# Down projection of a fused adaLN block: eight of its eleven pieces moved to float32r, with the widening of h on ScalarE

## The chip, the cores and the metric

The kernel runs on one core of a Trainium2 chip. The metric is the device time of one execution in microseconds, the median of several runs. The core has TensorE (PE in the profile; PEld is its loading of stationary operands), VectorE (DVE), ScalarE (ACT), GpSimd (POOL) and SyncE (SP). Each works through its own queue of instructions in order; transfers are issued from SP's or GpSimd's queue.

## The reference

The input x is two sequences of 4096 rows of 512 numbers (8192 rows in all). A transformer block is applied: a modulated layer norm, a gated linear recurrence over the sequence (the "attention" part), then a second modulated layer norm and a feed-forward part with 1408 inner columns. Every operand of the feed-forward matrix products is rounded to four bits in blocks of 16 along the contracted dimension.

```python
def fp4_linear(x, w):
    xq = fp4_quant_dequant(x)     # per block of 16: scale = max|x| / 6, value = grid[...] * sign * scale
    wq = fp4_quant_dequant(w)
    return einsum('bsk,nk->bsn', xq, wq)

h = layernorm(x) * (1 + ca) + sa
x = x + ga * attn(h)                                     # h @ W, sigmoid, scan along n, q * y
h = layernorm(x) * (1 + cb) + sb
gate, y = fp4_linear(h, w_gate), fp4_linear(h, w_up)     # 512 -> 1408 each
x = x + gb * fp4_linear(silu(gate) * y, w_down)          # 1408 -> 512
```

The six modulation rows sa, ca, ga, sb, cb, gb come from a small product of the condition vector c; there is one set for each of the two sequences (batches).

## The kernel before

The program has two phases. The first (0 to about 528 us) does the attention part, and beside it rounds the feed-forward weights and lays them in SBUF transposed: `wgT` and `wuT` (gate and up) and `wdT` (down). Every weight and every activation is held as two float16 parts, a high and a low one, and a product of two such numbers is made in passes of TensorE: three float16 passes (high x high, high x low, low x high; the list `PASSES`), or two passes where one part is made so that less is lost (the list `TWO`: high x high and low x low, with parts that are mixed by a factor, `LAM` or `LAMX`).

The second phase (528 us to the end) goes over `NT` = 64 tiles of 128 rows. The order of all instructions on every engine is the order in which the loop at the end writes them (`tc.manual_schedule`). Names below are those of `before.py`.

- `products(i)` (line 1069): gate and up of tile i. There are three column groups of 480, 464 and 464, each for two matrices, into six PSUM banks. The contracted 512 columns are four chunks of 128. `twos(i)` of these chunks are done in two passes with float32r weights (`wide`) and float32r activations (`xw`), the others in three float16 passes (`held` or `wgT`/`wuT`, with `x2T`). `twos` is 0 for the first tiles and climbs to 3 by one chunk every two tiles: tiles 5 and 6 have one, 7 and 8 two, later ones three. A group takes 12, 11, 10 or 9 passes accordingly, products 72, 66, 60 or 54.
- `down(i - LAG)`, with `LAG` = 2 (line 1190): the down product of the tile before last. The 1408 inner columns are eleven chunks ("pieces") of 128. The first eight take three float16 passes and the last three two (with `LAM`); this makes 30 passes of 512 columns into one of two side banks (`sd`). The stationary operand is h, transposed (`hT`); `wdT` streams.
- VectorE and ScalarE turn the products into h and quantise it. `silu` (line 1086, ScalarE) and `gated` (line 1091, VectorE) read the banks; VectorE's three gated products free them. Then follow the block maxima (`h_max`), the bounded scales (`sb`), a reciprocal of 88 columns, `h_unit` (division by the scale on VectorE, absolute values on ScalarE, line 1147), `h_round` (lines 107 and 109), and the parts. The first 1024 columns of h get theirs by one multiplication of the rounded integers with two spread scales (`h_spread` on ScalarE, line 1153, and line 1170 on VectorE); the last 384 get them by value: a multiplication (line 1164), a high part on ScalarE (line 1166), a low part (line 1176). One transpose on SP's queue writes `hT`.
- Between these steps lie those of later tiles: x of tile i + 2 is divided, rounded and transposed (`x_unit`, `x_round`, `x_low`; the transpose writes `x2T`), x of tile i + 3 is normalised (`x_hat` on ScalarE, `x_times` on GpSimd, `x_plus` on VectorE, its maximum and `x_scales`), and the statistics of tile i + 4 are taken (`mean_x`, `spread_x`, `x_off`). GpSimd also does the small scale steps (`total`, `h_scales`, `h_parts`).
- The output: `out_of` (line 1241, ScalarE) scales the side bank and frees it, `out_times` (line 1246, GpSimd) multiplies by gb, and `send` (line 1232) adds the result to the output in DRAM by a transfer on GpSimd's queue.
- At tile 0, `move_weights` (line 1018) copies gate and up weights to `held` in eight moves of 704 KB on SP's queue. From tile 2 to tile 7 one job per tile turns a half chunk (1408 columns) of them into float32r: `widen_sum` on VectorE, `widen_high` on ScalarE, `widen_low` on VectorE. The jobs for the chunks 3, 2 and 1 follow one another; `widen_rows` (line 1050, ScalarE) widens x.
- The start: x of tiles 0, 1 and 2 is brought on ahead in the slots of phase 1 (`EARLY`, `LATE`, `x_early` with its stages 0 to 3). The end: at tile 62 no down is queued; at tile 63 down(60) and down(61) stand behind products(63), then follow down(62) and `last_down(63)` in halves of 256 columns.

Of the kernel before, what the change touches and what calls it, by code (L numbers as in the profile page):

```python
# [19 lines left out]
P = 128  # L20
D = 512
# [23 lines left out]
LAM = 81.0  # L45
LAMX = 101.0
TWOS = 3
MOVED = 2


@with_exitstack
def tile_adaln_block(
# [62 lines left out]
    def bounded(engine, am, nb):  # L115
        sb = small.tile([P, nb], F32, name="sb", tag=f"sb{nb}", bufs=2)
        engine.tensor_scalar(sb, am, 6e-12, TIE / 6.0, ALU.max, ALU.mult)  # L117
        return sb
# [11 lines left out]
    def inverse(sb, nb):  # L130
        inv = small.tile([P, nb], F32, name="inv", tag=f"inv{nb}", bufs=2)
        V.reciprocal(inv, sb)
        return inv
# [272 lines left out]
    DOWN = [(k, *p) for k in range(IC) for p in (PASSES if k * P < HSPLIT else TWO)]  # L406
# [122 lines left out]
    def quant_weight(wt, am, col, parts, hl):  # L529
# [17 lines left out]
        for at, by in parts:  # L547
            if by is None:
                A.copy(b1[:, at], xn[:, at])
            else:  # L550
                A.activation(b1[:, at], xn[:, at], AF.Copy, scale=by)
# [3 lines left out]
    def quant_rows(wt, i, am, col):  # L555
        dst = weights(("wgT", "wuT")[col], col, [P, 2 * KC, INTER])
        hl = new_hl()
        yield from quant_weight(wt, am, col, [(slice(0, D), None)], hl)
        S.dma_start_transpose(dst[:, :, i * P : (i + 1) * P], flat(hl))
# [6 lines left out]
    def quant_down(wt, i, j):  # L566
# [5 lines left out]
        by = None if n0 < HSPLIT else (LAM - 1.0) / LAM  # L572
        yield from quant_weight(wt, am_d[i][j], 2, [(slice(0, w), by)], two)
# [52 lines left out]
    NS = NBLK * KC  # L626
    qx, x1s, xst, gbs = {}, {}, {}, {}
    mods = {}

    def mods_for(b):  # L630
        if b not in mods:
            mods[b] = (mod_load(4, b, f"mod_c{b}"), mod_load(3, b, f"mod_s{b}"))
        return mods[b]
# [13 lines left out]
    def spread_x(x1, nm):  # L647
        sq = work.tile([P, D], BF16, name="sq", tag="sq", bufs=1)
        ss = small.tile([P, 1], F32, name="vs", tag="vs")
        A.activation(sq, x1, AF.Square, bias=nm, accum_out=ss)  # L650
        rstd = small.tile([P, 1], F32, name="rstd", tag="rstd", bufs=10)
# [3 lines left out]

    def stats_x(x1):
        return spread_x(x1, mean_x(x1))

    def twos(i):
        return min(max((i - MOVED - 1) // 2, 0), TWOS)  # L660

# [10 lines left out]
    def x_scales(h, am):  # L672
        sb = bounded(G, am, NBX)
# [3 lines left out]
        return h, sb, st, u  # L677

    def x_unit(h, sb, st, u):
        xn = work.tile([P, D], F32, name="xn", tag="xn512", bufs=1)  # L680
        V.tensor_tensor(blocks(xn), blocks(h), spread(inverse(sb, NBX), NBX), ALU.mult)
        A.activation(h, xn, AF.Abs, scale=MAGIC)
        return h, xn, st, u
# [17 lines left out]

    ahead = {}

    def x_early(i, stage):
        if stage == 0:
            ahead[i] = x_scales(*x_norm(i))
        elif stage == 1:
            ahead[i] = x_unit(*ahead[i])
# [4 lines left out]

    EARLY = {NS - 3: [(0, 1)], NS - 2: [(0, 3), (1, 1)], NS - 1: [(1, 3)]}
    LATE = {NS - 4: [(0, 0)], NS - 3: [(0, 2), (1, 0)], NS - 2: [(1, 2)], NS: [(2, 0)]}

# [184 lines left out]
    with order:  # L901
# [3 lines left out]
        for slot in range(KC, NS + 3):  # L905
# [83 lines left out]
            if NS - 5 <= slot < NS - 1:  # L989
                n = slot - NS + 5  # L990
                xst[n] = stats_x(x1s[n])
            for n, stage in LATE.get(slot, []):
                x_early(n, stage)
            gate = cur
    tc.no_sync_barrier()
# [35 lines left out]
    def widen_sum(k, m):  # L1031
        hi, lo = moved[k][m]
        cv = ring.tile([P, INTER], F32, name="cv", tag="xnh")
        V.tensor_tensor(cv, hi, lo, ALU.add)
        return k, m, cv

    def widen_high(k, m, cv):
        A.copy(wide[k][m][0], cv)
        A.activation(cv, cv, AF.Copy, scale=LAMX)

    def widen_low(k, m, cv):
        b1, b2 = wide[k][m]
        V.scalar_tensor_tensor(out=b2, in0=b1, scalar=1.0 - LAMX, in1=cv, op0=ALU.mult, op1=ALU.add)

    def widen_rows(i):
        n = twos(i)
        if n:
            x2T = qx[i][0]
            xw = gring.tile([P, 2, n, P], F32R, name="xw", tag="xw", bufs=2)
# [29 lines left out]

    def brief():  # L1080
        return gring.tile([P, D], F32, name="silu", tag="silu", bufs=3)
# [18 lines left out]
    def x_off(i):  # L1100
        nm, rstd = xst[i]
        off = small.tile([P, 1], F32, name="off", tag="off")
        G.tensor_tensor(off, nm, rstd, ALU.mult)
        xst[i] = rstd, off

    def x_hat(i):
        rstd, off = xst.pop(i)
        h = x1s.pop(i)
        A.activation(h, h, AF.Identity, bias=off, scale=rstd)
        return i, h  # L1110

    def x_times(i, h):
        scale, by = mods_for(i * P // N)
        xm = brief()
        G.tensor_tensor(xm, h, scale, ALU.mult)
        return h, xm, by

    def x_plus(h, xm, by):
        V.tensor_tensor(h, xm, by, ALU.add)
# [4 lines left out]
    hb = HSPLIT // QB  # L1124

    def h_max(hid):
        am = small.tile([P, NBH], F32, name="amh", tag="amh", bufs=1)
        block_max(am, hid)
        return hid, bounded(V, am, NBH)

    def h_scales(sb):
        rt, u = total(sb, NBH, ud, 1)
        sl = small.tile([P, NBH], F32, name="sl", tag=f"sl{NBH}", bufs=2)
        G.tensor_scalar(sl[:, hb:], sb[:, hb:], rt, WPEAK * LAM, ALU.mult, ALU.mult)  # L1134
        G.tensor_scalar(sl[:, :hb], sb[:, :hb], rt, None, ALU.mult)
        return rt, sl, u

    def h_parts(sb, rt, sl):
        sh = small.tile([P, hb], BF16, name="sh", tag="shh", bufs=2)
        A.activation(sh, sb[:, :hb], AF.Copy, scale=rt)  # L1140
        G.tensor_tensor(sl[:, :hb], sl[:, :hb], sh, ALU.subtract)
        return sh

    def h_unit(hid, sb):
        xn = ring.tile([P, INTER], F32, name="xn", tag="xnh")
        V.tensor_tensor(blocks(xn), blocks(hid), spread(inverse(sb, NBH), NBH), ALU.mult)  # L1146
        A.activation(hid, xn, AF.Abs, scale=MAGIC)  # L1147
        return xn

    def h_spread(sh, sl):  # L1150
        se = ring.tile([P, 2, HSPLIT], F16, name="se", tag="se")
        for n, src in enumerate((sh, sl[:, :hb])):
            A.activation(blocks(se[:, n, :]), spread(src, hb), AF.Copy, scale=WPEAK)
            yield se
# [7 lines left out]
    def h_value(xn, nq, sl):  # L1162
        v = xn[:, HSPLIT:]
        V.tensor_tensor(blocks(v), blocks(nq[:, HSPLIT:]), spread(sl[:, hb:], NBH - hb), ALU.mult)
        hl = ring.tile([P, 2, INTER], F16, name="hhl", tag="hhl")
        A.activation(hl[:, 0, HSPLIT:], v, AF.Copy, scale=1.0 / LAM)
        return v, hl

    def h_low(i, nq, v, hl, se, u):
        V.tensor_tensor(  # L1170
            hl[:, :, :HSPLIT],
            nq[:, :HSPLIT].unsqueeze(1).to_broadcast([P, 2, HSPLIT]),
            se,
            ALU.mult,
        )
        V.scalar_tensor_tensor(
            out=hl[:, 1, HSPLIT:],
            in0=hl[:, 0, HSPLIT:],
            scalar=1.0 - LAM,
            in1=v,  # L1180
            op0=ALU.mult,
            op1=ALU.add,
        )
        hT = ring.tile([P, 2 * IC, P], F16, name="hT", tag="hT", bufs=2)
        S.dma_start_transpose(hT, flat(hl))
        qh[i] = hT, u

    def down_part(hT, pd, d):
        for n, (k, hp, wp) in enumerate(DOWN):
            T.matmul(  # L1190
                pd,
                hT[:, hp * IC + k, :],
                wdT[:, wd_chunk(wp, k), d],
                start=n == 0,
                stop=n == len(DOWN) - 1,
            )

    def down(i):
        hT, u = qh.pop(i)
        pd = side((P, D))  # L1200
        down_part(hT, pd, slice(0, D))
        return i, pd, u

    def last_down(i):

        hT, u = qh.pop(i)
        b, t0 = divmod(i * P, N)
        o = new_out()
        for n in range(2):
            d = slice(n * D // 2, (n + 1) * D // 2)  # L1210
            pd = bank(n)[:, : D // 2]
            down_part(hT, pd, d)
# [166 lines left out]
```

## Time and profile before

| | us |
|---|---|
| median of 3 runs | 1700.97 (1698.98 to 1703.94) |
| profiled execution | 1701.52 |
| its span | 1699.7 |
| phase 1, 0 to 528.6: busy PE / DVE / ACT / POOL | 526.7 / 442.1 / 399.3 / 297.9 |
| tiles 0 to 9, 528.6 to 719.2 (190.6) | 187.6 / 172.4 / 124.5 / 102.8 |
| tiles 10 to 61, 719.2 to 1643.8 (924.6) | 924.6 / 841.0 / 607.9 / 511.1 |
| the end, 1643.8 to 1699.7 (55.9) | 48.9 / 34.7 / 18.5 / 13.0 |

The span is one execution on the core; the profiled execution's own time is 1.8 us longer. A row of the profile names the line, the engine, the operation, the written and read tiles, their shapes and the number of instructions, then the busy time in us, the mean of one in ns, the idle time of that engine just before them and what ended it. Here float32r operands appear as f32 (matrix products) or fp32r (casts). In the chain of waits each row is a stretch of work on the path that ended last; in a timeline a row is a run of like instructions on one engine, with the idle time before it in brackets.

### The profile page before, as it was taken

Reading aid. Unit: us, or ns where it says so; the run is one execution under the profiler, and the core shown is the slowest. Engines: PE = TensorE matmul, PEld = TensorE weight load, DVE = VectorE, ACT = ScalarE, POOL = GpSimd, SP = SyncE. Lnnn points to the kernel's source line nnn. Section 1 sums busy time; section 2 is a strip of 40 time slices with the busy share of each in tenths; the row PEclk is TensorE's granted clock in tenths of the full one; section 3 lists DMA queues with packets and bytes.
Section 4 is the critical chain, followed back from the end, with each engine's and each line's share of the span. In section 5 each row is a group of like instructions: output and inputs, shape, how many; then the busy total and the mean of one; then the engine's idle time right before and its main releaser. Section 6 shows DMA issues by size and latency. Waiting matters only on the chain.

```text
span 1699.7 us, 24145 instructions
## 1 busy us (share of the span) xinstructions
PE 1687.7 (99%) x8089; PEld 944.2 (56%) x8089; DVE 1490.2 (88%) x1927; ACT 1150.2 (68%) x2295; POOL 924.8 (54%) x1277
## 2 busy tenths in 40 slices
PE   9999999999999999999999999999999999999998
PEld 6444444444444445565666666666666566665664
DVE  7767889899985999998989989899898998998985
ACT  6676787788875667766666666666666666666652
POOL 5554555566654455655555555555555555555532
PEclk9999999999999999999999999999999999999999
DMA  7799979999976534445444444444444444444444
GB/s 249 177 243 218 201 184 204 186 206 199 207 153 183 114 70 82 80 81 95 97 93 86 78 95 78 88 86 83 95 78 83 89 83 94 79 80 94 73 82 72
DMA packets 471453, 208.92 MB, mean 123 GB/s; under 512 B 426470, under 2 KB 427750, under 8 KB 471328
## 3 DMA queue, kind: packets, MB, share of 16 engines
q1 hardware_dynamic: 456496, 173.85, 48.5%
q0 software_dynamic: 14544, 33.52, 11.1%
q8 instruction: 63, 1.03, 0.2%
q14 instruction: 62, 0.51, 0.1%
q10 hardware_dynamic: 288, 0.01, 0.0%
HBM read 62.86 MB, written 33.58 MB: 57 GB/s over the span
## 4 chain that ended last, share of the span: by engine, by line
PE 94%; DMA 2%; DVE 2%; ACT 1%; issue 1%; POOL 0%; DVEq 0%; POOLq 0%; SPq 0%; ACTq 0%
PE mm L1069 43%; PE mm L417 27%; PE sd L1190 23%; DMA gmax<-gsum 1%; DMA hT<-hhl 1%; DMA xT<-hl 0%; PE mm L1190 0%; PE mm L819 0%; DMA x2T<-hl 0%; ACT sq L370 0%; PE sd L220 0%; PE sd L234 0%; DVE ld L158 0%; ACT hl L383 0%; DVE xn L107 0%
## 5 line engine op out<-in xcount | busy, mean ns | idle before, releaser
L1069 PE MATMUL mm<-wide,xw 128*128 128x464 f32 (+1 forms) x2052 | 553.9, 403 | 0.0
L417 PE MATMUL mm<-xT,wqT 128*128 128x512 f16 (+1 forms) x2340 | 498.4, 376 | 0.8 <-DMA xT<-hl 0.8
L1069 PEld LDWEIGHTS mm<-wide,xw 128*128 128x128 f32 x2052 | 386.5, 188 | 72.5
L1190 PE MATMUL sd<-wdT,hT 128*128 128x512 f16 x1890 | 418.7, 379 | 1.7 <-DVE o L1221 1.7
L417 PEld LDWEIGHTS <-wqT 128*128 128x128 f16 x2340 | 228.6, 98 | 270.3 <-issue 1.7
L1069 PE MATMUL mm<-held,x2T 128*128 128x464 f16 (+1 forms) x1386 | 337.4, 365 | 3.0 <-DMA x2T<-hl 3.0
L1190 PEld LDWEIGHTS <-hT 128*128 128x128 f16 x1950 | 186.0, 98 | 226.8 <-issue 15.1
L1069 PEld LDWEIGHTS <-x2T 128*128 128x128 f16 x1530 | 126.3, 98 | 169.2 <-issue 71.1
L1091 DVE SCALAR_TENSOR_TENSOR hid<-mm,u,silu 128x464 f32<-128x464 f32 (+1 forms) x192 | 128.8, 701 | 79.4 <-PE mm L1069 69.3
L125 POOL TENSOR_TENSOR rt<-rms,mone 128x1 f32<-128x1 f32 x128 | 72.9, 569 | 221.7 <-ACT asb L123 221.7
L1147 ACT ACTIVATE hid<-xn 128x1408 f32<-128x1408 f32 x64 | 88.1, 1377 | 114.4 <-DVE xn L1146 114.4
L1086 ACT ACTIVATE silu<-mm,u 128x464 f32<-128x464 f32 (+1 forms) x192 | 116.3, 644 | 34.0 <-PE mm L1069 32.9
L453 ACT COPY yh<-y 128x1024 uint16<-128x1024 uint16 x64 | 66.9, 1045 | 68.8 <-DVE y L446 58.1
L652 POOL TENSOR_SCALAR rstd<-vs 128x1 f32<-128x1 f32 x118 | 25.2, 213 | 161.0 <-ACT sq L650 160.4
L107 DVE SCALAR_TENSOR_TENSOR xn<-hid,xn 128x1408 f32<-128x1408 f32 x64 | 103.6, 1619 | 2.9 <-ACT hid L1147 2.9
L1146 DVE TENSOR_TENSOR xn<-hid,inv 128x1408 f32<-128x1408 f32 x64 | 104.0, 1626 | 2.2
L136 DVE TENSOR_REDUCE amh<-hid 128x88 f32<-128x1408 f32 x64 | 103.7, 1620 | 2.2
L123 ACT ACTIVATE asb<-sb 128x88 f32<-128x88 f32 (+1 forms) x128 | 31.3, 245 | 107.9 <-DVE sb L117 105.1
L109 DVE SCALAR_TENSOR_TENSOR nq<-hid,xn 128x1408 f16<-128x1408 f32 x64 | 103.6, 1618 | 0.1
L1246 POOL TENSOR_TENSOR silu<-o,mod 128x512 f32<-128x512 f32 x32 | 41.2, 1288 | 100.3 <-DVE hid L1091 100.3
L435 DVE TENSOR_TENSOR_SCAN y<-sig,cy,mm 128x512 f32<-128x512 f32 x56 | 71.1, 1269 | 24.5 <-PE mm L417 21.2
L1134 POOL TENSOR_SCALAR sl<-sb,rt 128x24 f32<-128x24 f32 x64 | 88.3, 1379 | 6.3
(153 smaller groups left out, 2727.3 us busy)
## 6 DMA issues: line engine op xcount, KB each, us to landing
ld<-out_dram SPq DMA_DIRECT2D x65, 256.0 KB, 2.9
xr<-in_L_attn_x_dram SPq DMA_DIRECT2D x64, 256.0 KB, 3.7
out_dram<-xr POOLq DMA_DIRECT2D x64, 256.0 KB, 3.5
out_dram<-silu POOLq DMA_DIRECT2D x60, 256.0 KB, 4.0
scratch<-in_L_wmod_dram SPq DMA_DIRECT2D x24, 256.0 KB, 4.7
ld<-in_L_ffn_w_gate_dram SPq DMA_DIRECT2D x22, 256.0 KB, 3.1
ld<-in_L_ffn_w_up_dram SPq DMA_DIRECT2D x22, 256.0 KB, 3.3
ld<-in_L_ffn_w_down_dram SPq DMA_DIRECT2D x16, 256.0 KB, 3.5
```

The costliest lines, as they stand in the source:

```text
L107: V.scalar_tensor_tensor(out=xn, in0=a, scalar=FLOOR, in1=xn, op0=ALU.max, op1=ALU.add)
L109: V.scalar_tensor_tensor(out=nq, in0=a, scalar=FLOOR, in1=xn, op0=ALU.max, op1=ALU.subtract)
L125: G.tensor_tensor(rt, rms, mone[:, :1], ALU.pow)
L136: V.tensor_reduce(am, src.rearrange("p (b k) -> p b k", k=QB), AX.X, ALU.max, apply_absolute_value=True)
L417: T.matmul(pp[:, t], wqT[e][:, wp, k, part, :], xT[:, xp * KC + k, t], start=n == 0, stop=n == 3 * KC - 1,)
L1069: T.matmul(pp[:, : n1 - n0], x2T[:, xp * KC + k, :] if k < k0 else xw[:, xp, k - k0, :], (rows_of(i, m, k) if k < k0 else wide[k][m])[wp][ ...
L1086: A.activation(sl[:, :w], pairs[j][0][:, :w], AF.Silu, scale=u[:, 0:1])
L1091: V.scalar_tensor_tensor(out=hid[:, n0:n1], in0=pairs[j][1][:, : n1 - n0], scalar=u[:, 1:2], in1=sl[:, : n1 - n0], op0=ALU.mult, op1=ALU.mult,
L1134: G.tensor_scalar(sl[:, hb:], sb[:, hb:], rt, WPEAK * LAM, ALU.mult, ALU.mult)
L1146: V.tensor_tensor(blocks(xn), blocks(hid), spread(inverse(sb, NBH), NBH), ALU.mult)
L1147: A.activation(hid, xn, AF.Abs, scale=MAGIC)
L1190: T.matmul(pd, hT[:, hp * IC + k, :], wdT[:, wd_chunk(wp, k), d], start=n == 0, stop=n == len(DOWN) - 1,)
```

## The change

The change touches the second phase.

- Down: for the first `DWIDE` = 7 tiles it is 33 float16 passes (eleven pieces, three passes each). From tile 7 on the last three pieces take three float16 passes (9, first in order) and the first eight take two float32r passes each (16), with `LAMX`. The stationary operand h of these eight is widened from float16 to float32r on ScalarE (`widen_h`, 128 x 2048 columns), queued right behind the absolute values of the following tile's h. There is one buffer, `hwT`.
- The down weights of the eight pieces are widened too: the widening jobs become eleven (`wide_jobs`), two per tile, and end in tile 7. Three of them store their result to DRAM (`far`), and `fetch_far`, on GpSimd's queue at the end of tile 8, brings five pieces (2.5 MB) back into the room of `wdT` (`near`); the three float16 pieces are copied aside before (`keep_rest`, 768 KB, on SP's queue).
- The ways in which h's parts are made are swapped: the first 1024 columns go by value (two multiplications, two high parts on ScalarE, two subtractions), the last 384 by spread scales. Two transposes (`hvT`, `hrT`) replace one. ScalarE's high parts stand last in its order of a tile.
- h's and x's scales share one tile (`cell`) and one reciprocal. The shift addition of x moves from VectorE to GpSimd. The small steps of GpSimd are reordered (`total` and `h_scales` ahead of `rstd_x` and `x_off`, the sending of the output later); `squares_x` moves ahead on ScalarE, `x_unit` ahead of `h_unit`, and both steps of `h_round` stand together, ahead of `x_low`.
- `twos` climbs by one chunk per tile: tile 4 has one, tile 5 two, tile 6 and later three. `xw` has one buffer in place of two.
- The modulation rows of batch 1 are loaded into the tiles of batch 0, at tile 29 (gb at tile 16).
- The start: x of tile 2 passes two more stages in phase 1's extra slot, and its last stage is queued right behind products(0), ahead of `move_weights`. The end: at tile 63 only down(60) is queued up front; tiles 61 and 62 are widened on ScalarE before tile 63's sums, and tile 63 after the outputs.

```diff
-    DOWN = [(k, *p) for k in range(IC) for p in (PASSES if k * P < HSPLIT else TWO)]
...
     def twos(i):
-        return min(max((i - MOVED - 1) // 2, 0), TWOS)
+        return min(max(i - MOVED - 1, 0), TWOS)
...
+    def fetch_far():
+        t = ctile([P, 5, 2, D], F32R, "near", tag="weights2")
+        n = 0
+        for f in far:
+            w = f.shape[1]
+            G.dma_start(t[:, n : n + w], f)
+            n += w
+        for j in range(5):
+            wide_d[2 + j] = [t[:, j, part, :] for part in range(2)]
+
+    def wide_jobs():
+        for k, m in ((3, 0), (3, 1), (2, 0), (2, 1)):
+            yield half(k, m)
+        yield pieces(6, 1, far[2])
+        for m in range(2):
+            yield half(1, m)
+        yield pieces(2, 2, far[0])
+        yield pieces(7, 1, None)
+        yield pieces(4, 2, far[1])
+        yield pieces(0, 2, None)
...
-            xw = gring.tile([P, 2, n, P], F32R, name="xw", tag="xw", bufs=2)
+            xw = gring.tile([P, 2, n, P], F32R, name="xw", tag="xw")
...
-        xm = brief()
-        G.tensor_tensor(xm, h, scale, ALU.mult)
-        return h, xm, by
-
-    def x_plus(h, xm, by):
-        V.tensor_tensor(h, xm, by, ALU.add)
+        G.tensor_tensor(h, h, scale, ALU.mult)
+        G.tensor_tensor(h, h, by, ALU.add)
+        return h
...
+    def h_value(i, xn, nq, sl):
+        by = (LAMX - 1.0) / LAMX if i >= DWIDE else 1.0
+        hl = ring.tile([P, 2, HSPLIT], F16, name="hv", tag="hv")
+        for n, at in enumerate(HALVES):
+            b = slice(n * HB // 2, (n + 1) * HB // 2)
+            V.tensor_tensor(blocks(xn[:, at]), blocks(nq[:, at]), spread(sl[:, b], HB // 2), ALU.mult)
+            A.activation(hl[:, 0, at], xn[:, at], AF.Copy, scale=by)
+        return hl
...
+    def h_low(i, xn, hl, hrT, u):
+        for at in HALVES:
+            V.tensor_tensor(hl[:, 1, at], xn[:, at], hl[:, 0, at], ALU.subtract)
+        tag = "hwT" if i < DWIDE and (DWIDE - i) % 2 else "hvT"
+        hvT = ring.tile([P, 2 * KV, P], F16, name="hvT", tag=tag)
+        S.dma_start_transpose(hvT, flat(hl))
+        qh[i] = [hvT, hrT, u]
+
+    def widen_h(i, tag="hwT"):
+        make = ctile if tag != "hwT" else lambda *a, tag: ring.tile(*a[:2], name=a[2], tag=tag)
+        hwT = make([P, 2 * KV, P], F32R, "hwT", tag=tag)
+        A.copy(hwT, qh[i][0])
+        qh[i][0] = hwT
...
+        for k in range(KV):
+            for hp, wp in PASSES if i < DWIDE else TWO:
+                w = wdT[:, wd_chunk(wp, k), :] if i < DWIDE else wide_d[k][wp]
+                steps.append((hvT[:, hp * KV + k, :], w))
...
+            rt, u = total(sb, NBH, ud, 1)
+            inv = inverse(cell, slice(0, None if x is not None else NBH))
+            hs = h_scales(sb, rt)
...
+            if x is not None:
+                x = x_unit(inv, *x)
+            xn = h_unit(hid, inv)
+            sh = h_parts(sb, rt, hs)
+            A.activation(hid, xn, AF.Abs, scale=MAGIC)
...
+            if DWIDE < i < NT - 2:
+                widen_h(i - 1)
             if x is not None:
                 x = x_round(i + LEAD, *x)
-            next(spreading)
+            se = h_spread(sh, hs)
...
+            if i == DWIDE + LAG - 1:
+                fetch_far()
+            if job is not None:
+                wide_low(*job)
+                job = None
+            if i + 1 >= MOVED:
+                job = next(jobs, None)
+                if job is not None:
+                    job = wide_sum(job)
```

## The prediction

> **What bounds the kernel now.** I read the page first: who is busy, and what the chain that ended last is made of.
>
> ```profile
> PE 1687.7 (99%) x8089; PEld 944.2 (56%) x8089; DVE 1490.2 (88%) x1927; ACT 1150.2 (68%) x2295; POOL 924.8 (54%) x1277
> PEclk9999999999999999999999999999999999999999
> PE 94%; DMA 2%; DVE 2%; ACT 1%; issue 1%; POOL 0%; DVEq 0%; POOLq 0%; SPq 0%; ACTq 0%
> L1069 PEld LDWEIGHTS mm<-wide,xw 128*128 128x128 f32 x2052 | 386.5, 188 | 72.5
> L1190 PEld LDWEIGHTS <-hT 128*128 128x128 f16 x1950 | 186.0, 98 | 226.8 <-issue 15.1
> ```
>
> TensorE bounds it at full clock. Next the chain of waits in order of time (start, length, what); the second phase is an alternation of `products(i)` and `down(i-2)`:
>
> ```profile
> 560.13 16.02 PE mm L1069 x72
> 582.63 14.26 PE mm L1069 x72
> 643.95 13.35 PE mm L1069 x66
> 682.63 12.30 PE mm L1069 x60
> 719.20 11.29 PE mm L1069 x54
> 1305.93 11.29 PE mm L1069 x54
> 1317.22 6.49 PE sd L1190 x30
> 1323.71 11.29 PE mm L1069 x54
> ```
>
> Nothing stands between them: a tile is 17.78 us of TensorE alone. The windows view of that tile (length, then busy PE, PEld, DVE, ACT, POOL), and from the timeline the only place where VectorE idles in it:
>
> ```profile
> 1305.77:1323.55 17.78, 17.78 (x85) 11.00 (x84) 16.15 (x21) 11.74 (x25) 9.86 (x14) 1.00 0.45 85
> ```
>
> ```profile
> 1317.33 0.70 DVE L1091 SCALAR_TENSOR_TENSOR hid<-mm,u,silu 128x464 f32<-128x464 f32 x1 [1.25 <-PE mm L1069]
> ```
>
> VectorE's own chain is thus 17.78 - 1.25 = 16.53 us: close behind, so it must be recounted too. ScalarE (11.74) and GpSimd (9.86) have more room. Two more views matter, the issues of transfers (KB, us from issue to landing) and TensorE's timeline at the end:
>
> ```profile
> held<-wuT SPq DMA_DIRECT2D x4, 704.0 KB, 9.1
> out_dram<-silu POOLq DMA_DIRECT2D x60, 256.0 KB, 4.0
> hT<-hhl SPq DMA_TRANSPOSE x64, 5.2
> ```
>
> ```profile
> 1666.18 13.12 PE L1190 MATMUL sd<-wdT,hT 128*128 128x512 f16 x60
> 1680.99 6.63 PE L1190 MATMUL sd<-wdT,hT 128*128 128x512 f16 x30 [1.69 <-DVE o L1221]
> 1689.05 6.72 PE L1190 MATMUL mm<-wdT,hT 128*128 128x256 f16 x60 [1.43 <-DMA hT<-hhl]
> ```
>
> The sum is made against the profiled execution: span 1699.7, 1701.5 us with 1.8 around it, 0.5 above the median 1700.97. What a measurement of this kernel can tell from no change is about 0.3%, 5.1 us.
>
> **Step 1: down, per tile.** Before, 30 float16 passes take 6.49 us: 216.3 ns each. After, from tile 7 on, there are 9 float16 and 16 float32r passes. No row shows a float32r pass at 512 columns; the gate and up products show them at 480 and 464 (469.3 in the mean). All-float16 products take 14.26/72 = 198.1 ns a pass. Each further chunk moved to float32r replaces 18 such passes by 12 and shortens products by 13.35 - 12.32 and 12.32 - 11.29, 1.03 us; so 12 float32r passes take 18 x 0.1981 - 1.03 = 2.54, 211.3 ns each, 13 more than float16 at that width. At 512: 216.3 + 13 = 229.5. Down becomes 9 x 0.2163 + 16 x 0.2295 = 5.62, plus 0.02 for the change of type: 5.64, less by 0.85. Bounds: 216 ns (no extra; 1.08 saved) and 250 ns (an extra two and a half times as large; 0.52 saved). I take 229.5, the nearest rows being this engine's own. Weight loads: 188 ns against 98 in the rows, hidden under 229.
>
> The Trainium skill, "TensorE: Matmul & The Clock Gate" (Weight-path perf modes), says fast weight load is not used for FP32, which speaks against this change. The rows agree in kind (188 against 98). If nothing covered the slower loads, that alone would cost 16 x 0.09 = 1.4 us a tile, and the gain would be a loss; the products' spacing, with 2052 such loads in it, shows them covered at this width.
>
> **Does another engine become the bound?** New tile: 17.78 - 0.85 = 16.93.
> - VectorE, by spacing (a dependent step costs its duration, an independent one 0.09 less): it loses the three old value steps (0.48 + 1.14 + 0.47 = 2.09), the shift addition of x (0.70) and one of two reciprocals (0.70 + 0.35 become about 0.94, 0.12 less), and gains two multiplications and two subtractions of 512 columns (4 x 0.60 = 2.40) and one step of 768 float16 columns (three eighths of the 1.22 us step: 0.46). 16.53 - 2.91 + 2.86 = 16.5. Slack 0.45.
> - ScalarE: minus two spreadings of 1024 (2.10) and one high part of 384 (0.52), plus spreadings of 384 (2 x 0.53), high parts of 512 (2 x 0.62) and the widening of h, 2048 columns. Casts of 768 and 1408 columns take 0.83 and 1.36 us; the same slope gives 1.90 (bounds: 1.4, the longest single step there, and 2.2, in proportion to 768). 11.74 - 2.62 + 4.20 = 13.3 of 16.93. The widening waits for hvT's transpose, issued in the tile before, and for the end of down(i-2), which comes 5.7 us after the products; it stands behind h's absolute values, which end 6.4 us or more after them, so it rarely waits. Behind it queue x's parts, the spreadings and `out_of`. What counts is the end: h's high parts are last on it, behind the widening, x's parts, `out_of` and `x_hat`. I count ScalarE ready for the first high part 12.3 us after the tile's third gated product and VectorE's value there at 12.9: a margin of 0.6.
> - GpSimd: the added addition costs 1.28, like its multiplication; 9.9 + 1.3, about 11.2. Queued behind it are rms and scales; VectorE's maximum of x comes two long steps later, so it hides.
>
> The Trainium skill, "SBUF — State Buffer" (Reading the diagram), lets GpSimd and VectorE exclude one another on a shared port, which could hand the moved addition's 1.28 back to VectorE. In the trace the 512-column multiplication runs beside VectorE's maximum with no idle entry there; by the rule VectorE's chain and the tile would be 17.8 and the gain nothing, by the trace it is 0.85.
>
> So TensorE stays the bound. From products(10) to products(62) there are 52 tiles: -44 us (bounds -56, -27). The shift and scale rows of batch 1, loaded once before tile 32 into rows still in use, hold VectorE some 4 us (a 256 KB row lands in 4.7); the six product banks cover it.
>
> **Step 2: tiles 0 to 9.** Downs 0 to 6 take 33 float16 passes: 7 x 0.65 = +4.5; down(7) -0.85; the faster ramp gives six more chunks, 6 x 1.03 = -6.2. TensorE's work: -2.5. The waits:
> - Start: products(2) waits today 2.99 us for x2T(2), at 560.13. That transpose now goes ahead of the eight weight moves on SP's queue, which start later; products(2) needs them. Eight land in about 19 us today, by 559.6. I take -1.5 (0 to -3).
> - Eleven widening jobs, two per tile, make VectorE the bound: a half costs 1.62 + 1.62, so two bring a tile to 16.5 + 6.5 = 23 against TensorE's 20 to 21. The low half of chunk 1 is finished only in tile 5 or 6, and products(6) needs it: +3.6 (0 to 6).
> - ScalarE is held by the second store's buffer, and VectorE behind it: +4 at products(9) (0 to 5).
> - `fetch_far` stands on GpSimd's queue after down(6) and brings 2.5 MB. Rows: 704 KB lands in 9.1 among others, 256 KB in 4.0 on that queue; eight moves of 5.6 MB ran at 296 KB/us, so 2.5 MB takes 8.5, with issue 11. Down(7) needs it after 9 passes and products(9): +8 stall (3 to 12).
> The Trainium skill, "DMA: Bandwidth & Descriptors" (Anatomy of one DMA), fits 2.0 us plus bytes over 436e3 per microsecond: an estimate of 8 us for the same, +5 instead of +8.
> Sum: -2.5 - 1.5 + 3.6 + 4 + 8 = +11.5 (+2 to +20).
>
> **Step 3: the end.** Only down(60) is queued ahead now; the widenings of tiles 61 and 62 stand on ScalarE before tile 63's sums and absolute values, and the second waits for hvT(62): VectorE's chain slips 4.4. Half-width passes: 18 x 0.112 + 32 x 0.188 (the load, longer than a 256-column stream) = 8.0 against 6.7: +1.3. The widening of tile 63: 1.9, of which its float16 passes cover 1.0: +0.9. The last transpose is 16 chunks of 22: 8.67 us less at most 2.4; I take -1.7. Sum +5 (3 to 8).
>
> **Total.** 1701.5 - 44 + 11.5 + 5 = 1674.
>
> **Rivals.**
> - (B) VectorE's chain, not TensorE, ends last: a period of 17.1 to 17.5. For: slack of 0.45 only. Against: every duration comes from a row. 52 x 0.17 to 0.57 more: 1683 to 1704.
> - (C) The float32r pass at 512 costs no more than float16: 1662. It breaks even at 264 ns ((6.49 - 16.5/52 - 1.97)/16); no row comes near.
> - (D) Slower: the hand-over of h's high parts. If ScalarE is ready later than VectorE by more than 0.6 us, VectorE waits, the gated products of the next tile slip and TensorE idles on its banks. With the slack gone at 1.05 more, the kernel is no faster from 1.4 to 1.6 us more than worked out (16.5 us of loss are spread over 52 tiles: period 17.46) and slower by 0.3% from 17.57. This happens if the widening takes 3.6 us, not 1.9. At 1 us beyond: 17.57 + 1 - 0.16, 1760. For: the margin is small, and many steps precede. Against: 3.6 us of idle on ScalarE per tile.
> - (E) The change does not do what it says: the built order has 25 passes a tile from down(7) on, so I give it no chance.
>
> **How the numbers follow.** My forecast 0.66, own range 1659 to 1691 (float32r -12/+17, the start -9/+9, the end -2/+3, not all at once); C 0.06; B 0.13; D 0.15. Faster than 1695.9: 0.66 + 0.06 + 0.08 of B = 0.80. The rest of B, 0.05, is the same; D is slower, above 1706.1. The range runs from 1657, below C, to 1700, taking in most of B and leaving D out.
>
> **What would show it.** Right: down at 5.6 us x25 between products of 11.29, VectorE idle before the third gated product, a tile of 16.9; VectorE or a transfer in the chain only before 730 and after 1640. Wrong: a tile above 17.1 with TensorE's idle put down to VectorE's gated product, or VectorE idle before the low parts, put down to ScalarE's high parts (D); a float32r pass over 240 ns; a stall before down(7) beyond 12 us, or none.

## The result, and the profile after

The changed kernel takes 1727.55 us in the median (1726.78 to 1728.91) against 1700.37 for the kernel before: a ratio of 1.0157, 95% interval 1.0140 to 1.0175. It is slower by 1.6%, where a gain of 1.6% was forecast. The profiled execution has a span of 1726.1 us, 26.4 more than before.

The page of the changed kernel, the same parts as were read of the kernel before:

```profile
PE 1663.5 (96%) x7784; PEld 998.7 (58%) x7784; DVE 1557.3 (90%) x1940; ACT 1229.8 (71%) x2431; POOL 1169.4 (68%) x1347
PEclk9999999999999998999999999999999999999999
PE 35%; POOL 34%; DVE 14%; ACT 8%; issue 7%; DMA 2%; SPq 0%; ACTq 0%; POOLq 0%; DVEq 0%
PE mm L420 27%; POOL sl L1198 6%; PE mm L1139 5%; POOL sl L1205 4%; POOL brief L1314 4%; POOL ld L1182 4%; POOL ld L1181 3%; DVE hv L1247 3%; DVE hid L1170 3%; POOL rstd L655 3%; POOL out_dram L1305 2%; PE sd L1271 2%; POOL cell L122 2%; ACT ld L718 2%; POOL rt L129 2%
```

TensorE's work did shrink, by 24 us. But it is 35% of the chain now, hardly more than phase 1's products (L420); GpSimd, which had no share before, has 34%. Where the time went is read best from the moment at which each tile's third gated product ends on VectorE (from the timeline, us from the start of the span; the last line is the end of the span):

| tile | before | after | difference |
|---|---|---|---|
| 1 | 560.1 | 560.9 | +0.8 |
| 9 | 715.0 | 729.3 | +14.3 |
| 10 | 731.4 | 752.6 | +21.2 |
| 29 | 1069.1 | 1089.7 | +20.6 |
| 30 | 1086.9 | 1111.2 | +24.3 |
| 60 | 1620.3 | 1644.7 | +24.4 |
| 62 | 1655.9 | 1677.8 | +21.9 |
| 63 | 1669.0 | 1691.7 | +22.7 |
| end | 1699.7 | 1726.1 | +26.4 |

So 21 us were lost in the first ten tiles and 3.7 at tile 30; tiles 61 and 62, with less work beside them, gave 2.5 back, and the end cost 4.5. In between, where 44 us were to be won, nothing was: the tile took 17.78 us before and takes 17.79 after. That the two agree is chance; the tile is now set by other engines.

The chain of waits of the changed kernel in a tile in the middle (start, length, what):

```profile
1305.69 1.28 POOL brief L1314
1306.97 1.26 POOL ld L1181
1308.30 1.29 POOL ld L1182
...
1310.79 2.27 POOL sl L1198
...
1318.18 0.78 POOL cell L122
...
1320.21 0.71 ACT ld L718
1321.47 0.56 DVE hv L1247
1322.68 0.72 DVE hid L1170
1323.48 1.28 POOL brief L1314
```

It is a ring: GpSimd's three long steps (output times gb, x times scale, x plus shift), its small steps, x's scale bound (`cell`), ScalarE's sums and `x_hat`, h's high and low parts, the next gated product, and GpSimd again. TensorE is not in it. The same tile on VectorE, in the timeline:

```profile
1304.90 1.93 DVE L1170 SCALAR_TENSOR_TENSOR hid<-mm,u,brief 128x480 f32<-128x480 f32 x3
1306.86 1.62 DVE L140 TENSOR_REDUCE amh<-hid 128x88 f32<-128x1408 f32 x1
1308.52 1.14 DVE L122 TENSOR_SCALAR cell<-amh 128x88 f32<-128x88 f32 x1
1321.47 1.29 DVE L1247 TENSOR_TENSOR hv<-xn,hv 128x512 f16<-128x512 f32 x2 [0.42 <-ACT hv L1233]
```

All three gated products run together: VectorE waits for no product any more. Its 88-column scale step takes 1.14 us now; in the kernel before it took 0.20:

```profile
1319.72 0.20 DVE L117 TENSOR_SCALAR sb<-amh 128x88 f32<-128x88 f32 x1
```

GpSimd's moved addition runs from 1308.30 to 1309.59, and the scale step, begun at 1308.52, ends at 1309.66, right behind it. At the end VectorE idles 0.42 us for ScalarE's high part. Its chain: 17.79 = 16.43 + 0.94 (held) + 0.42 (idle); b3 below shows the 16.43 without the hold. GpSimd's rows show that the holding goes both ways:

```profile
700.16 0.35 POOL L1198 TENSOR_SCALAR sl<-cell,rt 128x24 f32<-128x24 f32 x1
1308.30 1.29 POOL L1182 TENSOR_TENSOR ld<-ld,mod 128x512 f32<-128x512 f32 x1
1310.79 2.27 POOL L1198 TENSOR_SCALAR sl<-cell,rt 128x24 f32<-128x24 f32 x1
1315.58 1.62 POOL L1205 TENSOR_TENSOR sl<-sl,sh 128x24 f32<-128x24 f32 x1
1318.18 0.77 POOL L122 TENSOR_SCALAR cell<-amx 128x32 f32<-128x32 f32 x1
```

The 24-column scale step took 0.35 us in an early tile and 2.27 here, beside two of VectorE's divisions; it ends 0.14 us after the second of them. With this, x's scale bound comes at 1318.18, 13.3 us after the first gated product began, against 10.7 before (1325.5 from 1314.8). ScalarE's queue waits for it (1.23 us idle), and the high parts stand behind.

TensorE in the same tile:

```profile
1306.57 1.56 PE L1139 MATMUL mm<-wide,xw 128*128 128x480 f32 x6 [0.53 <-ACT xw L1120]
1317.35 2.12 PE L1271 MATMUL sd<-rest,hrT 128*128 128x512 f16 x9
1319.12 1.28 PE L1271 MATMUL sd<-part,hwT 128*128 128x512 f32 x4
1320.23 2.48 PE L1271 MATMUL sd<-near,hwT 128*128 128x512 f32 x10
1322.55 0.63 PE L1271 MATMUL sd<-part,hwT 128*128 128x512 f32 x2
1323.03 0.78 PE L1139 MATMUL mm<-held,x2T 128*128 128x480 f16 x3
```

Down goes from 1317.35 to 1323.03, 5.68 us, as forecast (5.64); products plus down are 16.99. Most of the other 0.80 is its wait for widened x, which stands on ScalarE behind the silu.

### The profile page after: what moved, and what is told of

Read it like the earlier page. It is cut to its first block, busy times and chain, and to the rows that moved or that the text cites. A ratio compares the mean times of both kernels' runs of the same rounds, so it can differ in the third digit from the quotient of the medians.

```text
span 1726.1 us, 23908 instructions
## 1 busy us (share of the span) xinstructions
PE 1663.5 (96%) x7784; PEld 998.7 (58%) x7784; DVE 1557.3 (90%) x1940; ACT 1229.8 (71%) x2431; POOL 1169.4 (68%) x1347
## 4 chain that ended last, share of the span: by engine, by line
PE 35%; POOL 34%; DVE 14%; ACT 8%; issue 7%; DMA 2%; SPq 0%; ACTq 0%; POOLq 0%; DVEq 0%
PE mm L420 27%; POOL sl L1198 6%; PE mm L1139 5%; POOL sl L1205 4%; POOL brief L1314 4%; POOL ld L1182 4%; POOL ld L1181 3%; DVE hv L1247 3%; DVE hid L1170 3%; POOL rstd L655 3%; POOL out_dram L1305 2%; PE sd L1271 2%; POOL cell L122 2%; ACT ld L718 2%; POOL rt L129 2%
## 5 line engine op out<-in xcount | busy, mean ns | idle before, releaser
L420 PE MATMUL mm<-xT,wqT 128*128 128x512 f16 (+1 forms) x2340 | 498.2, 376 | 1.4 <-DMA xT<-hl 1.4
L420 PEld LDWEIGHTS <-wqT 128*128 128x128 f16 x2340 | 228.7, 98 | 270.6 <-issue 2.4
L1314 POOL TENSOR_TENSOR brief<-o,mod 128x512 f32<-128x512 f32 x63 | 81.1, 1288 | 155.6 <-DVE hid L1170 146.3
L1271 PE MATMUL sd<-near,hwT 128*128 128x512 f32 x560 | 141.6, 399 | 8.0 <-DMA near<-far 8.0
L1198 POOL TENSOR_SCALAR sl<-cell,rt 128x24 f32<-128x24 f32 x64 | 138.2, 2159 | 6.6
L1170 DVE SCALAR_TENSOR_TENSOR hid<-mm,u,brief 128x464 f32<-128x464 f32 (+1 forms) x192 | 123.7, 698 | 5.4 <-PE mm L1139 3.5
L1271 PE MATMUL sd<-rest,hrT 128*128 128x512 f16 x504 | 119.9, 383 | 6.8 <-ACT o L1309 6.8
L1271 PEld LDWEIGHTS sd<-near,hwT 128*128 128x128 f32 x560 | 106.4, 190 | 34.0 <-DMA near<-far 9.1
L655 POOL TENSOR_TENSOR rstd<-rstd,mhalf 128x1 f32<-128x1 f32 x118 | 107.7, 913 | 9.8
L1256 ACT CAST hwT<-hvT 128x2048 fp32r<-128x2048 f16 x57 | 107.6, 1888 | 8.0 <-PE sd L1271 8.0
L1165 ACT ACTIVATE brief<-mm,u 128x464 f32<-128x464 f32 (+1 forms) x192 | 110.3, 643 | 3.8 <-PE mm L1139 3.8
L1271 PE MATMUL sd<-part,hwT 128*128 128x512 f32 x336 | 107.2, 427 | 0.0
```

Of the source, the lines that this page charges most:

```text
L420: T.matmul(pp[:, t], wqT[e][:, wp, k, part, :], xT[:, xp * KC + k, t], start=n == 0, stop=n == 3 * KC - 1,)
L655: G.tensor_tensor(rstd, rstd, mhalf[:, 0:1], ALU.pow)
L1165: A.activation(sl[:, :w], pairs[j][0][:, :w], AF.Silu, scale=u[:, 0:1])
L1170: V.scalar_tensor_tensor(out=hid[:, n0:n1], in0=pairs[j][1][:, : n1 - n0], scalar=u[:, 1:2], in1=sl[:, : n1 - n0], op0=ALU.mult, op1=ALU.mult,
L1198: G.tensor_scalar(sl[:, HB:], sb[:, HB:], rt, None, ALU.mult)
L1256: A.copy(hwT, qh[i][0])
```

## The experiments

Each ratio is to the kernel before, run again beside the experiment (medians 1701.8 for e1 to e4 and 1701.1 for b1 to b4). The tile is the time from one tile's third gated product to the next one's.

**e1: the shift addition back on VectorE.**

```diff
         G.tensor_tensor(h, h, scale, ALU.mult)
-        G.tensor_tensor(h, h, by, ALU.add)
-        return h
+        return h, by

-    def x_max(h):
+    def x_max(h, by):
+        V.tensor_tensor(h, h, by, ALU.add)
...
-                nx = x_max(nx)
+                nx = x_max(*nx)
```

> The shift addition of x goes back from GpSimd to VectorE, ahead of x's maximum; all else is as changed. Theory H (the hand-over through GpSimd sets the tile: its added addition and the small steps behind it make x's scales late, ScalarE waits for them with h's high parts queued behind, VectorE waits for the high parts, and the addition also holds up VectorE's 88-column scale step, 1.15 us instead of 0.20): the scale step is 0.2 again, ScalarE's high parts are ready when VectorE comes, and the tile is VectorE's own sum, 17.79 - 0.42 - 0.95 + 0.7 = about 17.1 us instead of 17.79; 52 tiles x 0.7 = 36 us less than the changed kernel, about 1690. Rival P (TensorE or the float32r passes set the tile): 17.79 stays. Rival S (ScalarE's widening of h makes the high parts late): 17.79 stays or grows by the added VectorE step, 18.4.

Measured: 1696.8 us, ratio 0.9971 (0.9960 to 0.9981). The tile is 17.14: theory H held, P and S did not. Timelines of VectorE and GpSimd:

```profile
1304.84 0.21 DVE L122 TENSOR_SCALAR cell<-amh 128x88 f32<-128x88 f32 x1
1308.24 0.69 DVE L1185 TENSOR_TENSOR ld<-ld,mod 128x512 f32<-128x512 f32 x1
1317.17 1.28 DVE L1247 TENSOR_TENSOR hv<-xn,hv 128x512 f16<-128x512 f32 x2
```

```profile
1310.26 0.23 POOL L1205 TENSOR_TENSOR sl<-sl,sh 128x24 f32<-128x24 f32 x1
```

The scale step is back at 0.21, the idle time before the low parts is gone, and the addition costs its 0.7: 16.43 + 0.7 = about 17.14. The idle time goes because VectorE's later steps now come 0.7 us later against GpSimd's: GpSimd's 24-column product takes 0.23 us in place of 1.62, x's scale bound comes 10.2 us after the first gated product in place of 13.3, and ScalarE is ready before VectorE is. One addition of 512 columns, moved to the less busy engine, had cost the kernel 31 us. TensorE's widened down is worth something now, but VectorE, without any idle time, is the bound.

**e2: GpSimd's order.** The output's multiplication is put behind h's scales, so that x's two steps would be done before VectorE's scale step.

```diff
-            outs = [out_times(*o) for o in scaled_out]
             nx = x_times(*hat) if hat is not None else None
...
             hs = h_scales(sb, rt)
+            outs = [out_times(*o) for o in scaled_out]
```

> On GpSimd the multiplication of the output by gb is queued behind h's scales, not ahead of x's multiplication and addition; GpSimd's work is the same. The addition then ends before VectorE's 88-column scale step starts. Theory H: that step takes 0.2 us instead of 1.15, all that follows on GpSimd starts 0.8 earlier, VectorE's chain is 16.4, and the tile falls to TensorE's 17.0 or close above (17.0 to 17.3): 1684 to 1702. Rival H' (the sum of GpSimd's steps alone makes x's scales late, the held step does not matter): the tile stays at 17.6 to 17.8. Rival P: 17.79 stays.

Measured: 1848.49 us, ratio 1.0859, tile 19.9. None of the three expectations held. VectorE and GpSimd in the timeline:

```profile
1308.90 0.21 DVE L122 TENSOR_SCALAR cell<-amh 128x88 f32<-128x88 f32 x1
1313.61 1.67 DVE L112 SCALAR_TENSOR_TENSOR hl<-ld,xn 128x512 f16<-128x512 f32 x1
1321.96 3.34 DVE L1247 TENSOR_TENSOR hv<-xn,hv 128x512 f16<-128x512 f32 x2 [0.41 <-ACT hv L1233]
```

```profile
1312.99 1.73 POOL L1314 TENSOR_TENSOR brief<-o,mod 128x512 f32<-128x512 f32 x1
1321.79 1.29 POOL L1181 TENSOR_TENSOR ld<-ld,mod 128x512 f32<-128x512 f32 x1
1323.15 1.60 POOL L1182 TENSOR_TENSOR ld<-ld,mod 128x512 f32<-128x512 f32 x1
```

The scale step is free (0.21), but the holding has moved: the steps that GpSimd's long steps now overlap are stretched, one rounding from 0.69 to 1.67 and the two low parts from 1.28 to 3.34. These two make up the whole difference: 0.98 + 2.06 - 0.93 (the freed scale step) = 2.11 us, and 17.79 + 2.11 = 19.90. The output's multiplication had waited for VectorE's first gated product (its buffer was read by it), and so kept GpSimd's long steps where VectorE does the gated products and the maximum, 1.93 + 1.62 = 3.6 us that nothing held. Two long steps (2.6 us) fit in there; three (3.9) do not.

**e3: h's high parts ahead on ScalarE.**

```diff
+            hl = h_value(i, xn, nq, hs)
             if nx is not None:
                 nx = x_scales(*nx)
             if not last:
                 scaled_out = [out_of(*e) for e in ended]
             hat = x_hat(i + LEAD + 2) if ahead_x else None
-            hl = h_value(i, xn, nq, hs)
```

> h's two high parts stand ahead of x's sums, the scaled output and the normalised x on ScalarE; all else is as changed. Theory H: VectorE's idle time of 0.42 us before the low parts goes; its chain with the held scale step is 17.37, so the tile is 17.4 and the kernel about 1706, if ScalarE's silu, now behind the other three, isn't late itself. Rival S (ScalarE has no room at the end of a tile): the silu come later by 1 us or more, VectorE waits for them before the gated products, and the tile stays at 17.8 or grows.

Measured: 1776.43 us, ratio 1.044, tile 18.74. The rival held, and by its mechanism:

```profile
1314.67 1.94 DVE L1170 SCALAR_TENSOR_TENSOR hid<-mm,u,brief 128x480 f32<-128x480 f32 x3 [1.40 <-ACT brief L1165]
```

The idle time before the low parts went, and 1.40 us came before the gated products: the high parts must wait for VectorE's values, and the sums, the output and `x_hat` then stand between them and the silu. Of the two places tried, last on ScalarE is the better one for the high parts, as long as what stands ahead of them is not late.

**e4: the widened down undone.** All pieces take three float16 passes in every tile (33), and no down weight and no h is widened.

```diff
-DWIDE = 7
+DWIDE = 64
...
-        yield pieces(6, 1, far[2])
         for m in range(2):
             yield half(1, m)
-        yield pieces(2, 2, far[0])
-        yield pieces(7, 1, None)
-        yield pieces(4, 2, far[1])
-        yield pieces(0, 2, None)
...
```

> Only the down part is undone, and more: all eleven pieces take three float16 passes (33 passes) in every tile, no down weight and no h is widened, nothing is stored and fetched back; order, ramp, start and end as changed. TensorE's tile is then 11.3 + 7.14 = 18.4, above the 17.79 of the hand-over: theory H gives 18.4 to 18.5, with TensorE never idle. On the early tiles: if the five added widening jobs on VectorE and the fetch cause the 14 + 7 us that tiles 2 to 10 lost against the kernel before, tile 9's third gated product comes at about 718 to 722 instead of 729 and tile 10's some 18 us later; if the start (x of tile 2, weight moves) causes it, it stays at 727 or more. In all 1736 to 1745.

Measured: 1738.26 us, ratio 1.0216 (1.0195 to 1.0236). The chain of waits in the middle is TensorE alone, 18.47 us a tile:

```profile
1310.16 11.33 PE mm L1134 x54
1321.49 7.14 PE sd L1266 x33
```

Tiles 6 to 15, in which VectorE makes up for its late start while TensorE has work in store, show the ring without the widening of h: 17.73 to 17.79 us each, with the scale step at 1.09 to 1.12 and the same idle 0.42 before the low parts. So neither the widening on ScalarE nor the float32r passes make the ring. And tile 9's third gated product comes at 717.8, as expected: 11.5 us earlier than in the changed kernel, which is the price of the five widening jobs of down with the copies and stores that belong to them. Tile 10 comes at 735.6, 17.0 earlier, with the fetch's wait gone too.

**b3: without the addition.** The shift addition of x is left out on every engine.

> The changed kernel without the shift addition of x on any engine (that part of the computation is left out). If the addition on GpSimd is the cause, and the count of VectorE's chain (16.4 to 16.5 us) was right, TensorE sets the tile: 16.99 (11.31 + 5.68), some 42 us less than 1727.5 over 52 tiles, 1685. If anything else is slow in the hand-over (the widening of h on ScalarE, the reordered small steps), the tile stays at 17.2 or more.

Measured: 1683.49 us, ratio 0.9895, tile 16.99, TensorE's own sum. From tile 31 to 52, after a wait at tile 30 that leaves TensorE ahead, the tile is 16.85: VectorE's 16.43 and the 0.42 before the low parts, which stay, as do GpSimd's held small steps:

```profile
1308.55 1.29 DVE L1246 TENSOR_TENSOR hv<-xn,hv 128x512 f16<-128x512 f32 x2 [0.42 <-ACT hv L1232]
```

```profile
1319.50 1.62 POOL L1204 TENSOR_TENSOR sl<-sl,sh 128x24 f32<-128x24 f32 x1
```

The count of VectorE's chain was right. The addition on GpSimd made the 0.94 us that the scale step was held, and with it 0.8 of the tile; it did not make the 0.42, which stand here without it.

**b4: the addition on GpSimd in the kernel before.** One part of the change alone.

```diff
         G.tensor_tensor(xm, h, scale, ALU.mult)
+        G.tensor_tensor(h, xm, by, ALU.add)
...
-        V.tensor_tensor(h, xm, by, ALU.add)
```

> The kernel before with one part of the change alone: the shift addition of x on GpSimd, behind its multiplication. VectorE starts its 88-column scale step there 1.25 us later than in the changed kernel against GpSimd's work, since it waits for TensorE before the third gated product; the three GpSimd steps end about 0.3 us before it. Theory (the addition harms only where it overlaps VectorE's steps and VectorE has no slack): the scale step stays at 0.2 to 0.5 us, the tile at TensorE's 17.78, the time at 1701 +- 3. Rival (the addition on GpSimd costs a tile wherever it stands, because x's scales come 1.3 us later): tiles above 17.9, 1708 or more.

Measured: 1701.0 us, ratio 0.9998 (0.9989 to 1.0007). VectorE and GpSimd:

```profile
1316.86 0.70 DVE L1091 SCALAR_TENSOR_TENSOR hid<-mm,u,silu 128x464 f32<-128x464 f32 x1 [1.50 <-PE mm L1069]
1317.59 1.62 DVE L136 TENSOR_REDUCE amh<-hid 128x88 f32<-128x1408 f32 x1
1319.25 0.21 DVE L117 TENSOR_SCALAR sb<-amh 128x88 f32<-128x88 f32 x1
```

```profile
1317.44 1.27 POOL L1116 TENSOR_TENSOR ld<-silu,mod 128x512 f32<-128x512 f32 x1
```

Here the addition ends at 1318.71, inside the maximum, and holds nothing: VectorE's wait for TensorE before the third gated product makes the unheld stretch longer. So the same edit is free where TensorE bounds the tile. The same run shows it where VectorE does, in tiles 10 to 13, while VectorE makes up for its late start:

```profile
769.17 1.09 DVE L117 TENSOR_SCALAR sb<-amh 128x88 f32<-128x88 f32 x1
```

The scale step is held there too, VectorE idles 0.38 us for ScalarE behind x's maximum, and a tile takes 17.07 us. With the addition on VectorE it took 16.43 (tile 10 of the kernel before). No part of the change of down is in this run: the place of the addition is enough.

**b2: the two loads earlier.** The changed kernel with the fetch of the widened pieces issued 13 us earlier and the modulation rows one tile earlier.

```diff
-            if i == NT // 2 - LEAD - 1:
-                mods_for(1)
...
             nx = x_times(*hat) if hat is not None else None
+            if i == DWIDE + LAG - 1:
+                fetch_far()
...
                 nx = x_max(nx)
+            if i == NT // 2 - LEAD - 2:
+                mods_for(1)
...
-            if i == DWIDE + LAG - 1:
-                fetch_far()
```

> The changed kernel with only the two earlier loads (fetched pieces, modulation rows). If the loads are costs of their own: tile 10's third gated product at about 746 instead of 752.6, tile 30 after 17.8 instead of 21.5; tiles stay at 17.79; 1727.5 - 7 - 3.7 = 1717. If GpSimd's hand-over swallows the gain: 1725 or more.

Measured: 1721.18 us, ratio 1.0117 (1.0097 to 1.0136), 6.4 less than the changed kernel where 10.7 were expected. Tile 10 comes at 747.9 (4.7 earlier, not 7, and tile 9 itself comes 0.8 later; at tile 12 3.8 are left), tile 30 after 17.78 (3.75 less). What they cost in the changed kernel, in the timelines of GpSimd and TensorE:

```profile
725.95 1.71 POOL L1080 DMA_DIRECT2D near<-far  x3
1094.52 1.46 POOL L1181 TENSOR_TENSOR ld<-ld,mod 128x512 f32<-128x512 f32 x1 [4.69 <-DMA mod<-modd]
```

```profile
733.58 2.08 PE L1271 MATMUL sd<-near,hwT 128*128 128x512 f32 x4 [7.40 <-DMA near<-far]
```

Down(6), the last reader of the room, ends at 712; the fetch is issued at 725.95, since it stands behind the whole tile's work on GpSimd's queue.

**b1: all three repairs together** (e1 and b2).

> Three edits together: the shift addition of x back on VectorE (as in e1_plus_vector, 1696.8 us), the fetch of the five widened pieces issued on GpSimd's queue right after x's multiplication in tile 8 (before: at the end of that tile, 14 us after the room came free), and the modulation rows of batch 1 issued in tile 28 right behind the last use of the old ones (before: in tile 29, behind the transposes of tile 28). Theory: TensorE's wait of 8.0 us for the fetched pieces goes nearly whole (-7), so does the wait of tile 30 (18.92 instead of 17.14, -1.8); tiles stay at 17.14: 1688. Rival: VectorE's chain is what is late at tile 10 anyway, and the fetch only hides it: -2 or less from the fetch, 1693 to 1695.

Measured: 1688.33 us, ratio 0.9921 (0.9907 to 0.9935): faster than both kernels, as expected. Tile 10 comes at 745.9 against 752.8 in e1, tile 30 after 17.14.

## Why the prediction was wrong

The forecast of 1674 missed by 53.5 us: from tile 10 to 62 the kernel won nothing (+0.7) where 44 were to be won, and the tiles before cost 21 where 11.5 were forecast.

- **Down's passes: right.** 5.68 us against 5.64; a float32r pass of 512 columns takes (5.68 - 9 x 0.2163)/16 = 0.233 us against 0.2295. The gain in TensorE's work was there, and b3 shows it as a tile of 16.99.
- **"TensorE stays the bound": this step failed**, through the bullet on GpSimd. The moved addition was priced at 1.28 us on GpSimd and at nothing on VectorE. It held VectorE's scale step for 0.94, twice the slack of 0.45: by e1, b3 and b4 that is what moved the bound from TensorE. A second term was mis-sized beside it, the margin at h's first high part. Counted from the end of the third gated product, ScalarE was to be ready after 12.3 us and VectorE's value after 12.9. In e1 they are, after 12.0 and 13.0. In b3 it is 13.1 against 12.2 and in the changed kernel 14.0 against 13.2, and VectorE idles 0.42 in both (without the hold TensorE still bounds the tile: 16.85 against 16.99 in b3). So the 0.42 come from taking the addition off VectorE, not from putting it on GpSimd: GpSimd's small steps then fall beside VectorE steps that hold them, and x's scales reach ScalarE late. GpSimd's busy time, in which held steps count at their full length, was put at 11.2 us a tile; in the windows view (length, then busy PE, PEld, DVE, ACT, POOL) it is 13.85:

```profile
1304.90:1322.68 17.78, 17.25 (x81) 11.81 (x80) 17.05 (x21) 12.95 (x27) 13.85 (x14) 1.00 0.49 85
```

- **The skill's rule was weighed and set aside wrongly.** The Trainium skill, "SBUF — State Buffer" (two separate sides), says that GpSimd and a VectorE operation with two SBUF inputs, or in a mode that uses both its ports, lock each other out for a whole instruction. I set against it a row in which GpSimd's multiplication runs beside VectorE's maximum. That was misread: in the tile shown it runs beside the third gated product (1316.81 to 1318.08; the maximum starts at 1318.07), and beside the maximum only in tiles where VectorE is late (715.10 beside 715.04). The maximum has one input, and the gated products read PSUM: these are what the runs show unheld. The scale step, a rounding and the low parts were held (0.20 to 1.14, 0.69 to 1.67, 1.28 to 3.34), and the divisions held GpSimd's 24-column step (0.35 to 2.27). Which of VectorE's steps the new one falls on had to be asked, not whether the two engines ever overlap. By the rule, the text put the tile at 17.8 and the gain at nothing. That number came true, in part by luck: it is 16.5 + 1.28, where the runs show 16.43 + 0.94 + 0.42.
- **VectorE's and ScalarE's own sums: right.** 16.43 against 16.5; the widening of h takes 1.89 us against 1.90, and ScalarE is busy 12.95 us of a tile against 13.3.
- **Rival D had the place and not the cause.** Its mechanism, high parts late on ScalarE, is in the ring, but it was tied to a widening of 3.6 us. The trigger was a wait ahead of the high parts, for GpSimd, which the text had not followed. Both of its signs came: a tile above 17.1 and VectorE idle before the low parts, for ScalarE. At 0.15 the chance for slower was too low for a VectorE slack of 0.45 us.
- **Modulation rows: "the six product banks cover it" failed.** It cost 3.75 us at tile 30, since TensorE had nothing in store; with VectorE as the bound (e1) it was still 1.8. Where TensorE is the bound, the step holds: in b3 tile 30 takes 19.98 us, and by tile 53 the 3.0 us are made up (407.7 us from tile 29 to 53, 24 x 16.99).
- **Tiles 2 to 9: mis-sized.** The text noted 23 us for a tile with two jobs on VectorE against TensorE's 20 to 21, and then took +3.6 and +4 for the waits. Tiles 3 to 7 measured 21.5 to 22.7, 2.0 to 2.9 above the kernel before each: +14.3 by tile 9, where the steps for these tiles sum to +3.6. Of this e4 shows 11.5 to be the five jobs; no run separates the other 2.8. TensorE's longest wait there is for the low half of chunk 1 in products(6), 8.14 us where +3.6 (0 to 6) was put, while products(9), given +4, begins without a wait:

```profile
656.27 2.37 PE L1139 MATMUL mm<-wide,xw 128*128 128x480 f32 x5 [8.14 <-DVE wide L1111]
```

- **The fetch: the wait right, its price not.** +8 was forecast, a wait of 7.40 + 0.58 us measured. But the passes right behind it run at a granted clock of 0.50 (windows view, 733.50 to 735.60 and 736.20 to 739.00), and down(7) takes 16.68 us (723.14 to 739.82) in place of 5.68. These further 3.0 us were in no step. The five passes above, behind the 8.14 us, ran at 0.50 too.
- **The end: right in sum** (+5 forecast, +4.5 from tile 62 on), but not in every part: the half-width passes were priced at the 188 ns of their weight load, and take 118. That is 2.2 us less for 32 of them, so the sum fits in part by luck.
- **Two sums of the rivals are off**, without weight for the result: by its own terms C breaks even at 263 ns, not 264, and D's 17.57 + 1 - 0.16 us a tile give about 1751, not 1760.

## What to carry to other kernels

Before moving a step from VectorE to GpSimd, lay it against the VectorE steps that it will run beside: in these runs GpSimd's steps were free beside reductions and PSUM readers, and stretched a scale step, a rounding and two subtractions by 0.9 to 2.1 us. An engine's idle time is not room for work if its steps can stop the engine that is about to become the bound. Taking a step off an engine also shifts all its later steps against the others': here that alone left ScalarE 0.42 us late. And where a change removes the bound's work, the waits that this bound had been hiding (a load issued a tile late, a fetch behind a full queue) all come due at once: list them, and issue those loads when their room comes free.

## What was not expected of the hardware

The recorded duration of a float32r weight load is 188 to 190 ns, but it does not limit the passes. In `last_down` of the changed kernel the float32r passes have 256 columns:

```profile
1717.74 1.35 PE L1271 MATMUL mm<-near,hwT 128*128 128x256 f32 x10
1718.92 0.40 PE L1271 MATMUL mm<-part,hwT 128*128 128x256 f32 x2
```

Ten of them take 1718.92 - 1717.74 = 1.18 us from start to start, 118 ns each, close to the 112 of the float16 ones at this width (6.72 us for 60 in the kernel before). And a step of 24 columns on GpSimd can take 0.35 or 2.27 us, by what VectorE is doing: the mean of a small GpSimd step says little of its cost in another place. The 2.27 us span two VectorE divisions, one right behind the other (1310.69 to 1311.38 and 1311.30 to 1312.92): the small step did not get in between them.
